# One kernel, four edits: GpSimd splits q and k, projections in one half turn, one dilation operation less, later transposes

## The chip, the cores and the metric

The kernel runs on one core of a Trainium2 chip. The time is the device time of one launch in microseconds (us); the median of several runs counts, and one further execution was recorded by the hardware profiler. The engines are named PE (matmul), PEld (its weight load), DVE (vector engine), ACT (scalar engine), POOL (GpSimd) and SP (which issues most DMAs). Each works through its own list of instructions in order and waits where one of them is not ready.

## What is computed

16 graphs of 1024 nodes with 128 features and a weighted 1024x1024 adjacency. Layer 0 is attention with 8 heads of 16, masked and weighted by the adjacency; layer 1 first thins the adjacency row by row ("dilation") and then runs three SAGE layers on it.

```python
# layer 0
h = relu(layernorm(x))
q, k, v = heads(h @ Wq.T + bq), heads(h @ Wk.T + bk), heads(h @ Wv.T + bv)
scores = where(adj == 0, -inf, q @ k.T / sqrt(16))
attn = softmax(scores) * adj
x = x + ((attn / (attn.sum(-1) + 1e-8)) @ v) @ Wo.T + bo
# layer 1, per graph, rows n in order
row = carry[n];  num = row.sum()
sf = (num + 1) // 2 if num > 10 else 1
rm = row & (cumsum(row) % sf == 0) & (num > 1)      # rows of nodes whose mask is set
carry[n] = row & ~rm;  carry[:, n] &= ~rm
# then, three times
agg = (adj_d @ h) / max(adj_d.sum(-1), 1)
o = agg @ Wr + h @ Wx + b;  h = batchnorm(relu(o / norm(o)))
x = x + concat(h1, h2, h3) @ Wl + bl
```

## The kernel before

**Two parts of one program.** `first_part` builds attention (a generator, `attention`) and dilation (a generator, `dilation`) and runs them interleaved in `beside_attention`; the SAGE layers follow in the loop over `L`, `b`, `c` below line 1275. PE, ACT and DVE execute in the order in which the Python code issues (a manual schedule), so where a line is called decides where it stands on its engine. Work for POOL and SP is issued in the same pass.

**A turn of attention** is (b, c, m): graph b, half c of the 512 query columns, block m of 128 key rows; 16 turns per graph, 256 in all. Each turn has two half turns g = 0 and 1, here called even and odd, four heads each. A half turn does, in this order:

1. `scores` (L596, L603): a mask product and the q-k products into two tiles of two banks, tag "sc". Float32 accuracy comes from q split in a rounded half `high` and a rest `low` (stacked in `qs`), and k in `ks` with alternate groups of 16 rows holding one or the other half.
2. even: `turn_over` (L547), the transposes of the adjacency block two turns ahead, into the one bank of tag "m".
3. `values` (L529, L534) for the half turn before, which needs its `w`.
4. the two exponentials `e` (L645) on ACT, one per score tile.
5. the two products `w = e * aT` (L650) on DVE.
6. even: the copy of the transposed block to `aT` (L550), which frees "m", and the mask `nomask` (L554).

**Steps beside it.** The next graph is prepared by generators kept in the list `beside`; each `yield` says where its next piece may go, and `go_on_with(kind)` at fixed places of a half turn lets the first generator that stands at that kind go on. `prepare(b)` does the layer norm, `turned` (transposes of h), and the projections: `key(c)`, `query(c)`, `value(c)`. `both_groups` (L349) makes a projection of two groups of heads, each with a matmul (L353) into tag "m" and a split:

```python
yield "end"                     # in prepare, ahead of key(0), query(0), key(1), query(1)
...
ps = where.tile([P, 512], F32, ...)        # both_groups, twice
nc.tensor.matmul(ps, wts[f"{name}{g}"], hT[:, c * HN : (c + 1) * HN], ...)
yield ("early", "evict")[g]
halves(c, g, ps)
if g == 0: yield "behind"
```

A step at "end" goes on at the close of an even half turn; "early" comes in the odd half turn ahead of `values`, "behind" after `values`, "evict" after the `w` products. For graph 0 the first two projections are made before the turns begin, with two banks. `query_halves` (L337, L338) and `key_halves` (L344, L345) read the projection out of PSUM twice: ACT writes the rounded half (for k it scales by `low_rows`, which is 1 for the rows of one kind and 0 for the others), DVE forms the rest from PSUM and that half.

**Dilation** works through 8 blocks of 128 rows, all graphs at once. At the end of a block, per graph: a running sum over pairs (`pair_sums`, L949, DVE); two ACT operations (L965) that turn it into distances from a threshold, one for even and one for odd places, written interleaved; a compare-and-maximum (L972) and a product with the row itself (L975), DVE; a maximum with earlier removals (L977); transposes (L956) and their copy (L958). The thresholds are small columns in `th` (L900 to L914).

**POOL** has the power of the layer norm (L302), the memset of `go_on` (L795), a small copy (L452), and the DMAs of the first rows (L504) and of the SAGE part.

**SAGE**: for each (L, b, c), `nodes` makes 64 sums in four pieces "sums", and the half before it (`before`) goes on between them with "scaled", "norm", "result", "transposed" (four transposes, L1225, and their copy, L1229). `turn_later` (L1344) decides whether "transposed" stands after the second or after the third piece. `judge` tests, once, that a sample is rounded alike by two engines.

Of the kernel before, what the change touches and what calls it, by code (L numbers as in the profile page):

```python
# [10 lines left out]
F32 = mybir.dt.float32  # L11
BF = mybir.dt.bfloat16
# [23 lines left out]
def swept(ctx: ExitStack, tc: tile.TileContext, t: dict, out: bass.AP, flag: bass.AP):  # L36
# [131 lines left out]
    def first_part(p1):  # L168
# [40 lines left out]
        wts |= {name: two_w[:, i, :] for i, name in enumerate(("q0", "q1", "k0", "k1"))}  # L209
        bqk = one.tile([P, 4, 2], F32, name="bqk")  # L210
        for i, name in enumerate(("L0_gnn_bq", "L0_gnn_bk")):
# [18 lines left out]
        def turn_weights():  # L230
            wps = ps_d.tile([P, 4, D], F32, name="wps", tag="d")
            for i in range(4):
                nc.tensor.transpose(wps[:, i, :], raw[:, i, :], ident)
            bps = ps_o.tile([P, HN], F32, name="bps", tag="acc0")
            for g in range(2):
                nc.tensor.matmul(
                    bps[:, 2 * g : 2 * g + 2], twice_ident[:, g, :], bqk[:, 0, :], start=True, stop=True
                )
            yield
            twofold(two_w[:, 2:4, :], wps[:, 3, :])  # L240
            twofold(two_w[:, 0:2, :], wps[:, 2, :])
            nc.vector.tensor_copy(one_w, wps[:, 0:2, :])
            nc.vector.tensor_copy(bqk[:, 1:3, :].rearrange("p g t -> p (g t)"), bps[:, 0:4])
            nc.vector.tensor_scalar(bqk[:, 3, :], bqk[:, 1:3, 1], low_rows, None, ALU.mult)
            yield
# [24 lines left out]
        free += 2 * (HN // 2 + 1)  # L270
        cx_home = both[:, free : free + HN]
        twice_ident = shared.tile([P, 2, P], F32, name="twice_ident", tag="s", bufs=2)
        twofold(twice_ident, ident)
# [38 lines left out]
        def prepare(b):  # L312
# [18 lines left out]

            def query_halves(c, g, ps):
                if g == 0:
                    qs.append(pool.tile([P, 2, 2, HN], F32R, name=f"q_{b}_{c}", tag="qM"))
                high, low = (qs[c][:, g, i, :] for i in range(2))
                bias = bqk[:, 1 + g, 0:1]
                nc.scalar.activation(high, ps, AF.Identity, bias=bias)  # L337
                nc.vector.scalar_tensor_tensor(low, ps, bias, high.bitcast(F32), ALU.add, ALU.subtract)  # L338

            def key_halves(c, g, ps):  # L340
                if g == 0:
                    ks.append(pool.tile([P, 2, HN], F32R, name=f"k_{b}_{c}", tag="kA", bufs=3))
                half = ks[c][:, g, :]
                nc.scalar.activation(half, ps, AF.Identity, bias=bqk[:, 3, g : g + 1], scale=low_rows)  # L344
                nc.vector.scalar_tensor_tensor(  # L345
                    half, ps, bqk[:, 1 + g, 1:2], half.bitcast(F32), ALU.add, ALU.subtract
                )

            def both_groups(name, halves, c, banks):  # L349
                for g in range(2):  # L350
                    where, tag = banks[g % len(banks)]
                    ps = where.tile([P, 512], F32, name=f"p{name}_{b}_{c}_{g}", tag=tag)
                    nc.tensor.matmul(  # L353
                        ps, wts[f"{name}{g}"], hT[:, c * HN : (c + 1) * HN], start=True, stop=True
                    )
                    yield ("early", "evict")[g]
                    halves(c, g, ps)
                    if g == 0:
                        yield "behind"
# [23 lines left out]
            if b == 0:  # L383
# [20 lines left out]
                yield from turned(1)  # L404
                yield "end"
                yield from key(1)
                yield True
                yield from value(1)
            else:
                yield from layer_norm_relu(h, xt, f"a{b}")  # L410
                for c in range(2):
                    yield True
                    yield from turned(c)
                yield "end"
# [4 lines left out]
                yield "end"  # L419
# [4 lines left out]
                yield "end"  # L424
                yield from key(1)
            yield "half 0"
            yield "end"
            yield from query(1)
# [93 lines left out]
        def attention():  # L522
# [87 lines left out]
            for i, (b, c, m) in enumerate(turns):  # L610
# [12 lines left out]
                for g in range(2):  # L623
                    scs = scores(i, g)
                    go_on_with(f"half {c}")
                    if g == 0:
                        go_on_with("first")
                        turning = turn_over(i + 2)
                        next(turning, None)
                    else:  # L630
                        twice_over = go_on_with("early")
                        if not twice_over:
                            go_on_with(True)
                    if late:
                        values(*late)
                        if g == 1 and twice_over:
                            go_on_with("behind")
                    elif g == 0:
                        go_on_with(True)
                    if (i, g) == (2, 0):  # L640
                        node_masks()
                    es, ws = [], []
                    for q in range(2):
                        e = pool.tile([P, 2, HN], F32, name=f"e_{b}_{c}_{m}_{g}_{q}", tag="e", bufs=4)
                        nc.scalar.activation(e, scs[q], AF.Exp, scale=1.0 / math.sqrt(HD))  # L645
                        es.append(e)
                    go_on_with("evict by VectorE")
                    for q in range(2):
# [11 lines left out]
                    go_on_with(False)  # L660
                    if g == 0 and next((kind for _, kind in beside if kind in (True, "end")), None) == "end":
                        go_on_with("end")
                    if i + g + 1 < len(turns):
# [8 lines left out]

        upto = one.tile([P, P], BF, name="upto")
        make_upper_triangular(nc, upto, 1.0, diag=True)
# [25 lines left out]
        def dilation():  # L700
# [84 lines left out]
            for k in range(NB):  # L785
# [29 lines left out]
                valid = shared.tile([P, B, P], BF, name=f"valid_{k}", tag="mr", bufs=4)  # L815
                cs = small.tile([P, 6, B], F32, name=f"cs_{k}", tag="cs", bufs=2)
                total, most, half, onw, last1, prev = (cs[:, i, :] for i in range(6))
# [81 lines left out]

                th = small.tile([P, 5, B], F32, name=f"th_{k}", tag="th", bufs=2)  # L900
                num, at_odd, off, allof, at_even = (th[:, i, :] for i in range(5))
                high = v[:, 3, :]
# [3 lines left out]
                nc.vector.tensor_scalar(high, num, 10.5, None, ALU.is_gt)  # L906
                nc.vector.scalar_tensor_tensor(allof, num, 1.5, high, ALU.is_gt, ALU.subtract)

                nc.vector.tensor_scalar(num, num, 0.5, 0.25, ALU.mult, ALU.add)
                nc.vector.tensor_scalar(num, num, MAGIC, MAGIC, ALU.add, ALU.subtract)  # L910
                nc.vector.tensor_scalar(at_odd, num, -3.0, None, ALU.mult)
                nc.vector.tensor_scalar(at_even, num, -3.0, 2.0, ALU.mult, ALU.add)
                nc.vector.scalar_tensor_tensor(off, num, 1.0, high, ALU.add, ALU.mult)
                nc.vector.tensor_scalar(off, off, -1.0, None, ALU.add)  # L914
                yield 2.0, 1
# [29 lines left out]
                for i in range(B + 2):  # L945
# [15 lines left out]
                    if b < B:  # L961
                        pairs[b] = shared.tile([P, 2, N], BF, name=f"pair_{k}_{b}", tag="mr", bufs=4)
                        wrs[b] = pairs[b][:, 0, :].bitcast(F16)
                        for t, at in enumerate((at_even, at_odd)):
                            nc.scalar.activation(  # L965
                                wrs[b][:, t::2], pair_sums[b % 2][:, t : t + HN], AF.Abs,
                                bias=at[:, b : b + 1], scale=2.0,
                            )
                    b = i - 1
                    if 0 <= b < B:  # L970
                        er = ers[b] = pairs.pop(b)[:, 1, :]
                        nc.vector.tensor_scalar(  # L972
                            er, wrs.pop(b), off[:, b : b + 1], allof[:, b : b + 1], ALU.is_equal, ALU.max
                        )
# [53 lines left out]
        def judge(sample):  # L1028
# [239 lines left out]
    with tc.manual_schedule(  # L1268
# [6 lines left out]
        for L in range(3):  # L1275
# [10 lines left out]
            for b in range(B):  # L1286
# [4 lines left out]
                for c in range(2):  # L1291
# [742 lines left out]
```

## Time and profile before

| | |
|---|---|
| median of 3 runs | 3463.39 us (3460.59 to 3468.24) |
| the profiled execution | 3457.88 us, of which the span of its instructions 3456.0 us |
| busy: PE, DVE, ACT, POOL | 3245.2, 3052.3, 2357.7, 165.0 us |
| granted TensorE clock | 0.991 |
| L650, product `w`, DVE | 1024 times, 1219 ns |
| L645, exponential `e`, ACT | 1024 times, 1022 ns |
| L353, projections, PE | 128 for k, 128 for q; 668 and 651 ns |
| L302, power, POOL | 33 times, shortest for 8 elements 1.64 us |

Busy times are sums over one engine; two engines can be busy at once. A row of the profile names the line, the engine, the operation and the tile that it writes and reads, with the shape. Matmul durations overlap, so that their mean is longer than the distance between two. A wait is an engine's idle time ahead of an instruction, put down to what came last; only a wait on the engine that is behind costs time.

### The profile page before, as it was taken

Reading aid. Unit: us, or ns where it says so; the run is one execution under the profiler, and the core shown is the slowest. Engines: PE = TensorE matmul, PEld = TensorE weight load, DVE = VectorE, ACT = ScalarE, POOL = GpSimd, SP = SyncE. Lnnn points to the kernel's source line nnn. Section 1 sums busy time; section 2 is a strip of 40 time slices with the busy share of each in tenths; the row PEclk is TensorE's granted clock in tenths of the full one; section 3 lists DMA queues with packets and bytes.
Section 4 is the critical chain, followed back from the end, with each engine's and each line's share of the span. In section 5 each row is a group of like instructions: output and inputs, shape, how many; then the busy total and the mean of one; then the engine's idle time right before and its main releaser. Section 6 shows DMA issues by size and latency. Waiting matters only on the chain. (4 is left out here: it accounts for less than half of the span.)

```text
span 3456.0 us, 86700 instructions
## 1 busy us (share of the span) xinstructions
PE 3245.2 (94%) x34987; PEld 1905.7 (55%) x34987; DVE 3052.3 (88%) x5410; ACT 2357.7 (68%) x3942; POOL 165.0 (5%) x253
## 2 busy tenths in 40 slices
PE   8998998999999899899999999999999899999997
PEld 3433333333343333333334334336999899999997
DVE  8888988988898898998999999997888799988887
ACT  7699789779879978977986996895323343432334
POOL 2000000000000000000000000001000000000000
PEclk9999999999999999999999999999999999999999
DMA  7356447537645735754773684577999799989997
GB/s 237 108 170 184 138 130 211 149 121 211 186 132 177 232 121 156 231 168 138 223 218 112 204 256 128 152 220 265 342 336 334 278 352 351 349 327 349 351 352 237
DMA packets 650124, 772.30 MB, mean 223 GB/s; under 512 B 173264, under 2 KB 569168, under 8 KB 637424
## 3 DMA queue, kind: packets, MB, share of 16 engines
q1 hardware_dynamic: 632672, 708.58, 63.1%
q0 software_dynamic: 15456, 57.30, 4.9%
q8 instruction: 276, 4.52, 0.6%
q14 instruction: 136, 1.11, 0.1%
q10 hardware_dynamic: 1584, 0.79, 0.1%
HBM read 508.50 MB, written 157.29 MB: 193 GB/s over the span
## 5 line engine op out<-in xcount | busy, mean ns | idle before, releaser
L650 DVE TENSOR_TENSOR w<-e,aT 128x1024 f32<-128x1024 f32 x1024 | 1205.9, 1219 | 135.3 <-ACT e L645 134.1
L645 ACT ACTIVATE e<-sc 128x1024 f32<-128x1024 f32 x1024 | 991.2, 1022 | 230.1 <-PE sc L603 229.6
L1188 PE MATMUL pg<-y,aT 128*128 128x128 f32 (+1 forms) x6144 | 730.5, 275 | 0.0
L1188 PEld LDWEIGHTS pg<-y,aT 128*128 128x128 f32 x6144 | 708.7, 192 | 0.0
L529 PE MATMUL acc<-w,both 128*32 128x512 f32 x4096 | 619.6, 610 | 4.5 <-DVE w L650 2.4
L534 PE MATMUL acc<-e,eps 128*32 128x512 f32 x4096 | 598.3, 594 | 0.0
L147 DVE SCALAR_TENSOR_TENSOR aT<-mr,aT 128x1024 f32<-128x1024 bf16 x384 | 458.8, 1217 | 0.0
L603 PE MATMUL sc<-q,k 32*128 32x512 f32 x4096 | 379.8, 445 | 0.0
L596 PE MATMUL sc<-nomask,never 32*32 32x512 bf16 x8192 | 272.8, 386 | 53.7 <-ACT e L645 46.8
L534 PEld LDWEIGHTS acc<-e,eps 128*32 128x32 f32 x4096 | 155.4, 111 | 299.5 <-issue 289.7
L596 PEld LDWEIGHTS <-never 32*32 32x32 bf16 x8192 | 86.8, 88 | 395.7 <-issue 376.8
L1211 ACT ACTIVATE sq<-o 128x512 f32<-128x512 f32 x96 | 60.6, 631 | 356.9 <-DVE o L1206 356.9
L1229 ACT COPY hT<-pt 128x512 f32<-128x512 f32 x96 | 56.3, 586 | 266.4 <-PE pt L1225 257.9
L603 PEld LDWEIGHTS sc<-q,k 32*128 32x128 f32 x4096 | 155.7, 183 | 117.1 <-issue 116.9
L547 PE MATMUL pa<-ident,a 128*128 128x128 f32 x1024 | 168.3, 287 | 46.6 <-DVE k L345 20.4
L965 ACT ACTIVATE pair<-both,th 128x512 f16<-128x512 f16 x256 | 204.8, 876 | 2.4 <-DVE both L949 2.3
L529 PEld LDWEIGHTS acc<-w,both 128*32 128x32 f32 x4096 | 97.3, 108 | 155.4 <-DVE w L650 77.3
L547 PEld LDWEIGHTS pa<-ident,a 128*128 128x128 f32 x1024 | 107.6, 141 | 135.2 <-issue 56.3
L554 ACT ACTIVATE nomask<-aT 128x512 bf16<-128x512 f32 x256 | 161.5, 631 | 8.1
L1206 DVE SCALAR_TENSOR_TENSOR o<-pg,rdeg,mine 128x128 f32<-128x128 f32 x384 | 108.1, 344 | 56.2 <-PE pg L1188 53.0
L949 DVE TENSOR_TENSOR_SCAN both<-rk 128x513 f16<-128x513 bf16 x128 | 155.9, 1218 | 0.0
L550 ACT COPY aT<-pa 128x512 f32<-128x512 f32 x256 | 152.5, 596 | 4.9 <-PE pa L547 4.5
(240 smaller groups left out, 4056.5 us busy)
## 6 DMA issues: line engine op xcount, KB each, us to landing
aT<-aT_d SPq DMA_DIRECT2D x94, 2048.0 KB, 9.7
mr<-mr_d SPq DMA_DIRECT2D x188, 512.0 KB, 6.0
aT_d<-aT SPq DMA_DIRECT2D x256, 256.0 KB, 3.8
a<-in_adj SPq DMA_DIRECT2D x253, 256.0 KB, 3.3
ad<-in_adj SPq DMA_DIRECT2D x112, 512.0 KB, 4.4
nomask<-nomask SPq DMA_DIRECT2D x512, 96.0 KB, 2.5
nomask<-nomask SPq DMA_DIRECT2D x512, 64.0 KB, 2.7
nomask<-nomask SPq DMA_DIRECT2D x512, 32.0 KB, 2.6
```

What stands on the lines that cost most here:

```text
L147: nc.vector.scalar_tensor_tensor(part, mrs[h][:, j : j + 2, :].rearrange("p j n -> p (j n)"), 0.0, part, ALU.is_equal, ALU.mult)
L529: nc.tensor.matmul(acc[g][32 * j : 32 * j + 32, :], v1[:, m, (2 * j + g) * HW : (2 * j + g) * HW + 32], ws[j // 2][:, j % 2, :], start=(m ...
L534: nc.tensor.matmul(acc[g][32 * j : 32 * j + 32, :], eps8, es[j // 2][:, j % 2, :], start=False, stop=(m == NB - 1),)
L547: nc.tensor.transpose(pa[:, k * P : (k + 1) * P], a[:, k, :], ident)
L554: nc.scalar.activation(nomask[:, 0, :], aT[:, 0, :], AF.Relu, bias=1.0, scale=-1e38, accum_out=zeros[:, i : i + 1])
L596: nc.tensor.matmul(scs[j // 2][to : to + 32, j % 2, :], never[rows, rows], nomask[rows, j, :], start=True, stop=False, tile_position=(32 * ...
L603: nc.tensor.matmul(scs[j // 2][:, j % 2, :], ks[m // HB][rows, g, mm], qs[c][rows, g, half, :], start=False, stop=(half == 1), tile_positi ...
L645: nc.scalar.activation(e, scs[q], AF.Exp, scale=1.0 / math.sqrt(HD))
L650: nc.vector.tensor_tensor(w, es[q], aT.to_broadcast([P, 2, HN]), ALU.mult)
L949: nc.vector.tensor_tensor_scan(pair_sums[b % 2], row[:, 0::2], row[:, 1::2], 0.0, ALU.add, ALU.add)
L965: nc.scalar.activation(wrs[b][:, t::2], pair_sums[b % 2][:, t : t + HN], AF.Abs, bias=at[:, b : b + 1], scale=2.0,)
L1188: nc.tensor.matmul(pg[:, i // 2, at : at + width], aT[:, j, i * P : (i + 1) * P], y[:, j, :width], start=(j == 0), stop=(j == NB - 1),)
```

## The change

- **Projections.** ACT makes one plain copy with bias, `whole` (one buffer), of each projection; the two halves are then made from it by the engine given to `halves`: POOL where "m" is the only bank, DVE for the first two projections of graph 0. For q these are a copy to the rounded type and a subtraction, for k a product with `low_rows` and a subtraction. The fourth column of `bqk` goes.
- **Placing.** The kind "end" goes; a projection begins like other steps in the odd half turn, after `scores`. "early" now stands behind the first of the two exponentials, in every half turn; `values` and "behind" follow the second. Both groups of a projection fall into one half turn.
- **Dilation.** ACT writes the even and the odd distances as two contiguous halves, with a per-row factor `twos` in place of 2.0; the thresholds are built from `twos` such that a row removed as a whole needs no maximum; compare and product with the row are one `scalar_tensor_tensor` that reads and writes every second element. `cs` and `th` have one buffer instead of two.
- **SAGE.** `turn_later` holds in layer 0 for both halves.
- `upto` lies in spare room of the tile `both`, and the sample in `judge` is rounded by POOL instead of ACT.

```diff
-            def query_halves(c, g, ps):
+            def whole(name, g, ps, bias):
+                x = small.tile([P, HN], F32, name=f"whole_{name}_{b}_{g}", tag="whole", bufs=1)
+                nc.scalar.activation(x, ps, AF.Identity, bias=bias)
+                return x
+
+            def query_halves(c, g, ps, engine):
...
-                bias = bqk[:, 1 + g, 0:1]
-                nc.scalar.activation(high, ps, AF.Identity, bias=bias)
-                nc.vector.scalar_tensor_tensor(low, ps, bias, high.bitcast(F32), ALU.add, ALU.subtract)
-
-            def key_halves(c, g, ps):
+                x = whole(f"q{c}", g, ps, bqk[:, 1 + g, 0:1])
+                engine.tensor_copy(high, x)
+                engine.tensor_tensor(low, x, high.bitcast(F32), ALU.subtract)
+
+            def key_halves(c, g, ps, engine):
...
-                nc.scalar.activation(half, ps, AF.Identity, bias=bqk[:, 3, g : g + 1], scale=low_rows)
-                nc.vector.scalar_tensor_tensor(
-                    half, ps, bqk[:, 1 + g, 1:2], half.bitcast(F32), ALU.add, ALU.subtract
-                )
+                x = whole(f"k{c}", g, ps, bqk[:, 1 + g, 1:2])
+                engine.tensor_scalar(half, x, low_rows, None, ALU.mult)
+                engine.tensor_tensor(half, x, half.bitcast(F32), ALU.subtract)
...
-                    halves(c, g, ps)
+                    halves(c, g, ps, nc.gpsimd if len(banks) == 1 else nc.vector)
...
-                yield "end"
+                yield True
                 yield from key(1)
...
                     else:
-                        twice_over = go_on_with("early")
-                        if not twice_over:
-                            go_on_with(True)
-                    if late:
-                        values(*late)
-                        if g == 1 and twice_over:
-                            go_on_with("behind")
-                    elif g == 0:
                         go_on_with(True)
-                    if (i, g) == (2, 0):
-                        node_masks()
                     es, ws = [], []
                     for q in range(2):
                         e = pool.tile([P, 2, HN], F32, name=f"e_{b}_{c}_{m}_{g}_{q}", tag="e", bufs=4)
                         nc.scalar.activation(e, scs[q], AF.Exp, scale=1.0 / math.sqrt(HD))
                         es.append(e)
+                        if q == 0:
+                            go_on_with("early")
+                    if late:
+                        values(*late)
+                        go_on_with("behind")
+                    elif g == 0:
+                        go_on_with(True)
+                    if (i, g) == (2, 0):
+                        node_masks()
...
-                    if g == 0 and next((kind for _, kind in beside if kind in (True, "end")), None) == "end":
-                        go_on_with("end")
...
-                cs = small.tile([P, 6, B], F32, name=f"cs_{k}", tag="cs", bufs=2)
+                cs = small.tile([P, 6, B], F32, name=f"cs_{k}", tag="cs", bufs=1)
...
-                nc.vector.scalar_tensor_tensor(allof, num, 1.5, high, ALU.is_gt, ALU.subtract)
+                nc.vector.scalar_tensor_tensor(twos, num, 1.5, high, ALU.is_gt, ALU.subtract)
+                nc.vector.tensor_scalar(twos, twos, -2.0, 2.0, ALU.mult, ALU.add)
...
-                nc.vector.tensor_scalar(at_odd, num, -3.0, None, ALU.mult)
-                nc.vector.tensor_scalar(at_even, num, -3.0, 2.0, ALU.mult, ALU.add)
+                nc.vector.scalar_tensor_tensor(at_odd, num, -1.5, twos, ALU.mult, ALU.mult)
+                nc.vector.tensor_tensor(at_even, at_odd, twos, ALU.add)
                 nc.vector.scalar_tensor_tensor(off, num, 1.0, high, ALU.add, ALU.mult)
-                nc.vector.tensor_scalar(off, off, -1.0, None, ALU.add)
+                nc.vector.scalar_tensor_tensor(off, twos, -0.5, off, ALU.mult, ALU.add)
...
-                                wrs[b][:, t::2], pair_sums[b % 2][:, t : t + HN], AF.Abs,
-                                bias=at[:, b : b + 1], scale=2.0,
+                                wrs[b][:, t * HN : (t + 1) * HN], pair_sums[b % 2][:, t : t + HN], AF.Abs,
+                                bias=at[:, b : b + 1], scale=twos[:, b : b + 1],
...
-                        nc.vector.tensor_scalar(
-                            er, wrs.pop(b), off[:, b : b + 1], allof[:, b : b + 1], ALU.is_equal, ALU.max
+                        nc.vector.scalar_tensor_tensor(
+                            er.rearrange("p (i t) -> p t i", t=2), wrs.pop(b).rearrange("p (t i) -> p t i", t=2),
+                            off[:, b : b + 1], rk(b, 2, N + 2).rearrange("p (i t) -> p t i", t=2),
+                            ALU.is_equal, ALU.mult,
                         )
-                        nc.vector.tensor_tensor(er, er, rk(b, 2, N + 2), ALU.mult)
...
-            nc.scalar.copy(rounded[:, 0], sample)
+            nc.gpsimd.tensor_copy(rounded[:, 0], sample)
...
-                    turn_later = before and c == 0 and b > 0
+                    turn_later = before and (c == 0 or L == 0)
```

More of the change, by code (lines that the diff above doesn't have):

```diff
@@ L209, in first_part @@
         wts |= {name: two_w[:, i, :] for i, name in enumerate(("q0", "q1", "k0", "k1"))}
-        bqk = one.tile([P, 4, 2], F32, name="bqk")
+        bqk = one.tile([P, 3, 2], F32, name="bqk")
         for i, name in enumerate(("L0_gnn_bq", "L0_gnn_bk")):
@@ L243, in turn_weights @@
             nc.vector.tensor_copy(bqk[:, 1:3, :].rearrange("p g t -> p (g t)"), bps[:, 0:4])
-            nc.vector.tensor_scalar(bqk[:, 3, :], bqk[:, 1:3, 1], low_rows, None, ALU.mult)
             yield
@@ L271, in first_part @@
         cx_home = both[:, free : free + HN]
+        upto_home = both[:, free + HN : free + HN + P // 2].bitcast(BF)
         twice_ident = shared.tile([P, 2, P], F32, name="twice_ident", tag="s", bufs=2)
@@ L413, in prepare @@
                     yield from turned(c)
-                yield "end"
+                yield True
                 yield from key(0)
@@ L418, in prepare @@
                 yield "half 1"
-                yield "end"
+                yield True
                 yield from query(0)
@@ L423, in prepare @@
                 yield from value(1)
-                yield "end"
+                yield True
                 yield from key(1)
             yield "half 0"
-            yield "end"
+            yield True
             yield from query(1)
@@ L670, in attention @@
             ready["last"] = conclude(*done)
-        upto = one.tile([P, P], BF, name="upto")
+        upto = upto_home
         make_upper_triangular(nc, upto, 1.0, diag=True)
@@ L896, in dilation @@
                             nc.tensor.matmul(g, final[:, b, :], vb[:, 1, b, 0:1], start=False, stop=True)
-                th = small.tile([P, 5, B], F32, name=f"th_{k}", tag="th", bufs=2)
-                num, at_odd, off, allof, at_even = (th[:, i, :] for i in range(5))
+                th = small.tile([P, 5, B], F32, name=f"th_{k}", tag="th", bufs=1)
+                num, at_odd, off, twos, at_even = (th[:, i, :] for i in range(5))
                 high = v[:, 3, :]
```

## The prediction

> **What bounds the kernel now.** First the busy times by stage, with the stretch borders read from the timeline: up to 2385 us attention and dilation run interleaved, after that the three SAGE layers.
>
> ```profile
> 20.00:2385.00 2365.00, 2200.00 (x25948) 877.79 (x25947) 2134.93 (x3520) 1979.18 (x3151) 108.71 (x142) 0.99 0.58 175
> 2385.00:3456.00 1071.00, 1033.65 (x9015) 1022.20 (x9014) 906.27 (x1839) 370.77 (x777) 46.25 (x85) 0.98 0.92 331
> ```
>
> Columns: stretch, length, then busy us of PE, PEld, DVE, ACT, POOL, clock, DMA share, GB/s. In the second stage PE is busy 97% and nothing of it is touched but one transpose position. In the first PE (93%) and DVE (90%) both carry it, ACT has 84%, and POOL is empty (5%). [...]I take DVE as the first bound and ask where DVE and PE still wait. The waits of that stage answer:
>
> ```profile
> DVE w L650 <- ACT e L645: 134.1, 188, 2.8
> PEld pk L353 <- ACT aT L550: 60.5, 31, 3.6
> PEld pq L353 <- ACT aT L550: 45.4, 31, 2.6
> DVE k L345 <- ACT k L344: 34.8, 34, 3.3
> PEld pa L547 <- DVE k L345: 33.6, 31, 1.2
> PEld pa L547 <- DVE q L338: 33.1, 31, 1.2
> DVE q L338 <- ACT q L337: 18.4, 25, 2.3
> ```
>
> (total us, times, longest.) Nearly all but the first line belong to the q and k projections: the first of two matmuls waits at the end of an even half turn for ACT to empty the one "m" bank, and the next turn's transposes (`pa`) wait for DVE to empty it again. What that costs shows in the period between the `w` pairs (L650 starts in the timeline, means over batches 1 to 15, by the m of the turn, period / DVE busy, us):
>
> ```
> m      even half    odd half     carries
> 0      6.25/4.68    5.67/5.17    key(1), and the copies of acc
> 1      5.05/4.68    5.60/5.41    query(1)
> 12     4.86/3.81    5.08/4.46    key(0)
> 14     5.04/3.93    5.06/4.46    query(0)
> 2,3,5  4.27/4.16    4.60/4.35    no projection
> 8      4.64/4.11    4.53/4.17    the copies of acc
> ```
>
> Elsewhere DVE is 97% busy in even half turns; in those with a projection it idles 0.4 to 1.6 us.
>
> **Projections: removed.** The rows that are replaced (line, operation, count, busy us, mean ns):
>
> ```profile
> L344 ACT ACTIVATE k<-pk,bqk,low_rows 128x512 fp32r<-128x512 f32 x64 | 50.0, 781 | 39.1 <-PE pk L353 39.1
> L345 DVE SCALAR_TENSOR_TENSOR k<-pk,bqk,k 128x512 fp32r<-128x512 f32 x64 | 47.8, 747 | 37.1 <-ACT k L344 37.0
> L338 DVE SCALAR_TENSOR_TENSOR q<-pq,bqk,q 128x512 fp32r<-128x512 f32 x64 | 47.7, 745 | 18.4 <-ACT q L337 18.4
> L337 ACT ACTIVATE q<-pq,bqk 128x512 fp32r<-128x512 f32 x64 | 44.1, 690 | 40.7 <-PE pq L353 40.7
> ```
>
> Of 128 groups the first four (batch 0) go to DVE with two instructions each; 124 leave it. The next DVE start follows such an operation by 0.66 us, so DVE loses 124 x 0.67 = 83 us, 1.34 per pair of groups, 62 pairs. ACT keeps one evict per group at the 690 of L337 and saves 64 x 0.09 = 6.
>
> **Projections: moved.** Both groups now run in one odd half turn: first matmul behind the scores, its evict between the two exponentials, second matmul behind the values, its evict last. "m" was emptied half a turn before, so both kinds of bank wait go. Even half turns should fall to their neighbours: 6.25 to 4.64, and 5.05, 4.86, 5.04 to about 4.2, which is 1.6+0.9+0.7+0.8 = 4.0 us per batch. Projection steps issue no DMA.
>
> **Projections: added on POOL.** Two instructions per group, 248 in all. No POOL row of this size exists. The memsets of L795 (128x2048, 1805 ns) and L796 (128x16, 197 ns) give 0.17 us + 0.8 ns per element: 0.58 us for the one-input step. For two inputs I count the element cost twice, 0.99; the Trainium skill (GPSIMD Engine Reference, Performance versus the Vector engine) measures 4497 ns at 2048 elements, by its 2.6 cycles an estimated 1.17. I take 1.0. Then what they do to DVE. The trace has one reading POOL instruction beside a busy DVE:
>
> ```profile
> 1272.91 1.22 DVE L885 TENSOR_TENSOR hit<-w,at 128x2048 bf16<-128x2048 f16 x1
> 1273.14 2.48 POOL L302 TENSOR_TENSOR rs_b<-rs_b,minus_half 128x8 f32<-128x8 f32 x1 [31.10 <-DVE rs_b L301]
> 1274.04 2.36 DVE L650 TENSOR_TENSOR w<-e,aT 128x1024 f32<-128x1024 f32 x2
> ```
>
> L302 takes 1.64 at its shortest. Here it took 0.84 more, just what L885 had left; then the `w` pair ran at its usual length beside it. So POOL waits for a DVE operation with two SBUF inputs, and DVE was not held. The rule speaks against this change: the Trainium skill (SBUF — State Buffer, Who interferes with whom) has a DVE instruction with two SBUF inputs and a GpSimd instruction that reads SBUF exclude each other, the loser blocked for the whole instruction. The row contradicts "whole instruction", but its 8 elements are read at once; 512 are read throughout. By the row the hold H of a pair (four POOL instructions) is 0; by the rule 2 x (0.58+1.17) = 3.5 us, more than the 1.34 saved. I take 2.0: the two subtractions hold DVE fully, the two one-input steps fall where DVE waits anyway, because the evict between the exponentials makes the second one 0.69 us later.
>
> Pair time after = DVE busy before - 1.34 + H + 0.3 of waits that stay, but never under what is left without any hold: the even half turn of the neighbours plus an odd one of 5.0 (before 5.06 to 5.67; 0.6 us of matmul more, 1.34 of DVE less), 9.6 at m=0 and 9.2 else:
>
> ```
> m     before  DVE busy  H=0   H=2.0  H=3.5
> 0     11.92   9.85      9.6   10.8   12.3
> 1     10.65   10.09     9.2   11.05  12.55
> 12    9.94    8.27      9.2   9.25   10.75
> 14    10.10   8.39      9.2   9.35   10.85
> sum   42.61             37.2  40.45  46.45
> ```
>
> Times 15.5 batches: -84, **-33** and +60 us.
>
> **The new buffer.** `whole` has one buffer, so the second evict waits on ACT until POOL has read the first copy twice: 0.58 + 1.0 + a mean POOL wait of 0.4 before each (L302's excess over 1.64) = 2.4 us after the first evict; the second matmul is ready 1.5 after it. ACT stands 0.9 us, and the next exponential is queued behind. In a pair with H=2.0 DVE is behind by more than that, so I count nothing; without that cover it costs 0.4 to 0.9 per pair (25 to 55 us). Also behind POOL's new work: the power L302, which stands between the last copy and the last subtraction of query(1) (DVE's L304 waits for it one half turn later), the memset of go_on, and in batch 0 six first-row loads; +2 us in all.
>
> **Dilation.** L972 (536 ns) and L975 (693) become one operation; start of the first to start of the follower is 1.30 us. L765 with two bf16 inputs takes 1083 at 896 elements, so 1.22 at 1024, 1.26 with the same dependence: 128 x 0.04 = -5. Bounds: 1.14 as between independent operations (-20), and +20 if reading every second element cost DVE what it seems to cost ACT. ACT's L965 (876 ns) writes halves contiguously but takes a second pointer; L1152, that form, takes 805: 256 x 0.07 = 18 us of ACT, worth nothing, since DVE never idled for L965. One more tiny operation per block: 8 x 0.17 = +1. Single buffers for `cs`, `th`: their readers are done a block earlier, nothing.
>
> **Later turn.** In layer 0 the transposes of odd halves move behind one more set of sums. `PEld pt L1225 <- DVE o L1221: 4.6, 15` in that layer goes: -4; nothing is due soon behind it. The copy that goes to POOL in the final test runs once: 0 to 3.
>
> **Sum.** -33 + 2 - 5 + 1 - 4 = -39 on the profiled 3457.88 (span 3456.0): 3419. The median of the runs shown is 5.5 higher; I put the time at **3420**.
>
> **Rivals.**
> - **No hold** (H=0), chance 0.2: -84, +25 for the stand on ACT that no DVE backlog covers, -6 for the rest: about 3393. For it: the undelayed `w` beside L302. Against: that reads 8 elements.
> - **Full hold, slower**, 0.25: each POOL instruction shuts DVE out for its length, H=3.5: +60-6, about 3512. The pairs break even near H=2.5, so it decides from 0.64 us of hold per POOL instruction. For it: POOL demonstrably waits for DVE, and at m=0 and 1 DVE has little idle time to give.
> - **The `whole` wait replaces the bank wait**, 0.15: POOL, waiting for DVE twice, needs 4 us, ACT stands 2.5 us, and the even half turn's gain goes back: about 3455.
> - The forecast, 0.4: 3395 to 3445.
>
> **Numbers.** The range 3375 to 3500 holds the forecast, the no-hold and the buffer case; the full hold spreads over 3470 to 3530, and a bit over half of it is left out. Faster: all of no hold, 0.37 of the forecast's 0.4, half of the buffer case: 0.64. Within 0.2% (7 us, about what can be told from no change) 0.08; slower 0.28.
>
> **What would show it.** POOL rows of 0.6 and 1.0 us plus waiting; even half turns at m=1, 12, 14 near 4.2; no wait of `pk`, `pq` for `aT`; `w` rows longer than 1219 ns, or idle DVE put down to POOL, if it is held; `whole` waiting for POOL on ACT. POOL rows over 1.5 us with odd half turns over 6 would make it wrong.

## The result, and the profile after

The changed kernel takes **3510.82 us** (median of 4 runs, 3508.95 to 3518.39), the kernel before on the same chip 3464.73 (4 runs): a ratio of 1.0138, 95% interval 1.0119 to 1.0157. It is slower by some 46 us. The forecast of 3420 is missed by 91 us, and the range of 3375 to 3500 too. The profiled execution of the changed kernel took 3518.39 us with a span of 3516.5 at a granted clock of 0.984.

The stages first, by the view that the prediction began with. The border now lies at 2443 us, because the last product `w` ends at 2439.2 instead of 2378.4. Columns: stretch, length, busy us of PE, PEld, DVE, ACT, POOL, clock, DMA share, GB/s.

```profile
20.00:2443.00 2423.00, 2247.25 (x25921) 884.89 (x25921) 2178.06 (x3275) 1964.42 (x3151) 486.08 (x389) 0.98 0.57 170
2443.00:3516.00 1073.00, 1034.22 (x9041) 1025.88 (x9039) 909.79 (x1842) 371.16 (x777) 47.62 (x87) 0.98 0.91 331
```

All the loss is in the first stage, 58 us longer; the SAGE stage is as long as it was. POOL has gone from 109 to 486 us there. DVE, which was to be relieved, is busy 43 us more.

Where that comes from stands in the groups of operations on POOL and DVE (busy us, mean ns of one, idle time before it):

```profile
L350 POOL TENSOR_SCALAR k<-whole_k,low_rows 128x512 fp32r<-128x512 f32 x62 | 121.9, 1966 | 562.6 <-ACT whole_k L334 562.6
L343 POOL TENSOR_TENSOR q<-whole_q,q 128x512 fp32r<-128x512 f32 x62 | 115.1, 1857 | 3.8
L351 POOL TENSOR_TENSOR k<-whole_k,k 128x512 fp32r<-128x512 f32 x62 | 83.7, 1350 | 4.9
L342 POOL CAST q<-whole_q 128x512 fp32r<-128x512 f32 x62 | 55.8, 901 | 237.3 <-ACT whole_q L334 237.3
```

```profile
L653 DVE TENSOR_TENSOR w<-e,aT 128x1024 f32<-128x1024 f32 x1024 | 1261.4, 1269 | 199.8 <-ACT e L639 198.3
...
L974 DVE SCALAR_TENSOR_TENSOR pair<-pair,th,rk 128x1024 bf16<-128x1024 f16 x128 | 200.4, 1566 | 0.0
```

The POOL steps take 0.9 to 2.0 us where 0.58 and 1.0 were counted. The products `w` have grown from 1219 to 1269 ns in the mean; of the 1024 none took over 1.3 us before, and now 84 do, 27 of them about 2.3. All 84 run beside one of the POOL steps: DVE is held inside its instruction. And DVE waits 198.3 us for exponentials, before 134.1.

Why the exponentials come late is in the waits (us in total, times, longest; the last line is that of the attention stage alone):

```profile
DVE w L653 <- ACT e L639: 198.3, 219, 4.2
...
ACT whole_k L334 <- POOL k L351: 82.8, 31, 4.3
ACT whole_q L334 <- POOL q L343: 72.4, 29, 3.8
PEld pa L551 <- ACT whole_k L334: 57.1, 31, 3.5
PEld pa L551 <- ACT whole_q L334: 47.1, 30, 2.3
...
PEld pk L357 <- ACT aT L554: 9.1, 15, 0.8
```

The bank waits of `pk` and `pq` for `aT` are nearly gone, but in nearly every pair ACT now stands 2.6 us in front of the second evict until POOL has read the first copy twice. Behind that evict stand the next exponentials on ACT and the next turn's transposes (`pa`), which need the bank: they wait 104 us, where before they waited 67 for DVE to empty it. One pair in the timeline (start, duration, engine, line; idle time and its cause in brackets):

```profile
1046.60 0.69 ACT L334 ACTIVATE whole_k<-pk,bqk 128x512 f32<-128x512 f32 x1
...
1047.39 1.87 POOL L350 TENSOR_SCALAR k<-whole_k,low_rows 128x512 fp32r<-128x512 f32 x1 [24.64 <-ACT whole_k L334]
...
1049.35 1.28 POOL L351 TENSOR_TENSOR k<-whole_k,k 128x512 fp32r<-128x512 f32 x1
...
1050.66 0.69 ACT L334 ACTIVATE whole_k<-pk,bqk 128x512 f32<-128x512 f32 x1 [2.46 <-POOL k L351]
1051.24 1.93 ACT L639 ACTIVATE e<-sc 128x1024 f32<-128x1024 f32 x2
...
1051.44 1.56 POOL L350 TENSOR_SCALAR k<-whole_k,low_rows 128x512 fp32r<-128x512 f32 x1 [0.82 <-ACT whole_k L334]
...
1052.30 3.44 DVE L653 TENSOR_TENSOR w<-e,aT 128x1024 f32<-128x1024 f32 x2 [2.24 <-ACT e L639]
...
1053.09 1.56 POOL L351 TENSOR_TENSOR k<-whole_k,k 128x512 fp32r<-128x512 f32 x1
```

Read downwards it is one chain: first evict, two POOL steps, second evict after 2.46 us of standing, exponentials, and DVE, idle for 2.24 us, begins its `w` pair; that pair then takes 3.44 us in place of 2.35, while the second group's POOL steps run beside it (1051.44 to 1054.65).

The periods between `w` pairs, read as in the prediction (period / DVE busy, us, means over batches 1 to 15):

```
        before                     after
m       even half   odd half       even half   odd half
0       6.25/4.68   5.67/5.17      4.56/3.96   7.16/5.44
1       5.05/4.68   5.60/5.41      4.74/4.64   6.77/5.88
12      4.86/3.81   5.08/4.46      3.53/3.14   6.94/5.03
14      5.04/3.93   5.06/4.46      3.73/3.29   7.15/5.46
```

The even half turns fell as forecast. The odd ones took it back: a pair takes 1.94 us more than DVE's busy time (44.58 less 36.84 over four pairs, divided by four), where 0.3 was counted. The even half turns just behind a pair, at m=2 and m=13, rose too, from 4.17 and 3.79 to 5.06 and 4.15: POOL is still at work on the pair there and holds `w`.

### The profile page after: what moved, and what is told of

The parts are those of the page before. It is cut to its first block, busy times and chain, and to the rows that moved or that the text cites. A ratio compares the mean times of both kernels' runs of the same rounds, so it can differ in the third digit from the quotient of the medians.

```text
span 3516.5 us, 86951 instructions
## 1 busy us (share of the span) xinstructions
PE 3292.3 (94%) x34987; PEld 1916.4 (54%) x34987; DVE 3099.3 (88%) x5169; ACT 2343.1 (67%) x3941; POOL 543.8 (15%) x502
## 5 line engine op out<-in xcount | busy, mean ns | idle before, releaser
L653 DVE TENSOR_TENSOR w<-e,aT 128x1024 f32<-128x1024 f32 x1024 | 1261.4, 1269 | 199.8 <-ACT e L639 198.3
L533 PE MATMUL acc<-w,both 128*32 128x512 f32 x4096 | 647.0, 620 | 12.9 <-DVE w L653 10.0
L538 PE MATMUL acc<-e,eps 128*32 128x512 f32 x4096 | 624.0, 605 | 0.0
L147 DVE SCALAR_TENSOR_TENSOR aT<-mr,aT 128x1024 f32<-128x1024 bf16 x384 | 458.9, 1217 | 0.0
L600 PE MATMUL sc<-nomask,never 32*32 32x512 bf16 x8192 | 280.7, 386 | 67.4 <-ACT e L639 61.8
L350 POOL TENSOR_SCALAR k<-whole_k,low_rows 128x512 fp32r<-128x512 f32 x62 | 121.9, 1966 | 562.6 <-ACT whole_k L334 562.6
L974 DVE SCALAR_TENSOR_TENSOR pair<-pair,th,rk 128x1024 bf16<-128x1024 f16 x128 | 200.4, 1566 | 0.0
L967 ACT ACTIVATE pair<-both,th 128x512 f16<-128x512 f16 x256 | 195.0, 818 | 4.1 <-DVE both L951 4.1
```

The lines of the kernel that those rows point to most:

```text
L147: nc.vector.scalar_tensor_tensor(part, mrs[h][:, j : j + 2, :].rearrange("p j n -> p (j n)"), 0.0, part, ALU.is_equal, ALU.mult)
L533: nc.tensor.matmul(acc[g][32 * j : 32 * j + 32, :], v1[:, m, (2 * j + g) * HW : (2 * j + g) * HW + 32], ws[j // 2][:, j % 2, :], start=(m ...
L538: nc.tensor.matmul(acc[g][32 * j : 32 * j + 32, :], eps8, es[j // 2][:, j % 2, :], start=False, stop=(m == NB - 1),)
L600: nc.tensor.matmul(scs[j // 2][to : to + 32, j % 2, :], never[rows, rows], nomask[rows, j, :], start=True, stop=False, tile_position=(32 * ...
L653: nc.vector.tensor_tensor(w, es[q], aT.to_broadcast([P, 2, HN]), ALU.mult)
L967: nc.scalar.activation(wrs[b][:, t * HN : (t + 1) * HN], pair_sums[b % 2][:, t : t + HN], AF.Abs, bias=at[:, b : b + 1], scale=twos[:, b : ...
```

## The experiments

Two theories stood against each other. **W**: the wait of the second evict for the one `whole` buffer makes the kernel slow. **H**: POOL's reading holds DVE, buffer or not. A third, **D**, put it on the dilation. The kernel before ran beside each group, at 3460.3 to 3461.0 us, so times of different groups can be set side by side to about a microsecond; beside the changed kernel itself it stood at 3464.7, and a few us of each difference to 3510.82 are uncertain. For the space of the second buffer or a spare tile, e1, e6, e9, e10, e11 and e14 leave out the record of the denominators and its test (L452 before, 13 us on POOL, which has room); what that alone is worth was not measured.

**A second `whole` buffer (e1).**

```diff
-  x = small.tile([P, HN], F32, name=..., tag="whole", bufs=1)
+  x = small.tile([P, HN], F32, name=..., tag="whole", bufs=2)
```

> The changed kernel (3511 us) with two buffers for whole; room comes from leaving out the record rden of the denominators and its test. Theory W (ACT stands in the odd half turn until POOL has read the single copy, 155 us of waits in the trace of the changed kernel): those waits go, odd half turns with a projection fall from 7.0 to about 5.5, time about 3420 to 3440. Theory H (POOL's reading holds DVE, so DVE sets the pair): DVE is as busy as before, time 3485 to 3510. Theory D (the joined dilation operation, 1566 instead of 536+693 ns): no change, 3505 to 3515.

Measured 3458.73 us (20 runs; ratio to before 0.9989, 0.9982 to 0.9995), so the one buffer costs **52 us**. (e3 below, which keeps the one buffer and ran beside e1, stands 53 us over it.) Its waits:

```profile
DVE w L651 <- ACT e L637: 128.2, 162, 3.4
...
ACT whole_q L333 <- PE pq L356: 54.4, 35, 6.3
ACT whole_k L333 <- PE pk L356: 33.7, 35, 2.1
```

No `whole` waits for POOL, and DVE's wait for exponentials has fallen from 198.3 to 128.2, by 70 us, while DVE is held more than in the changed kernel (busy 3119.3 against 3099.3). W names the largest part, but its 3420 to 3440 was not reached: something else costs 20 to 40 us more.

**The halves by ACT and DVE again, all else changed (e2).**

```diff
-  x = whole(f"q{c}", g, ps, bqk[:, 1 + g, 0:1])
-  engine.tensor_copy(high, x)
-  engine.tensor_tensor(low, x, high.bitcast(F32), ALU.subtract)
+  nc.scalar.activation(high, ps, AF.Identity, bias=bias)
+  nc.vector.scalar_tensor_tensor(low, ps, bias, high.bitcast(F32), ALU.add, ALU.subtract)
   (k likewise)
```

> The changed kernel with the halves made by ACT and DVE out of PSUM as before; placing, dilation and later turn as changed. W and H both say that all of the loss goes: both name POOL. Even half turns stay near 4.0 as in the changed kernel, odd ones return to 5.1 to 5.6: about 3400 to 3430, below the kernel before. D says that the loss stays: about 3500.

Measured **3434.59 us**, ratio 0.9927 (0.991 to 0.9944): faster than the kernel before, and the fastest of all that ran, if 5 us above the range expected: its even half turns with a projection take 4.7 to 5.7 us, not 4.0. Making the halves on POOL costs 76 us against that, 52 by the one buffer and 24 even with two.

**The dilation alone, both ways (e3, e4).** e3 is the changed kernel with the dilation operations of before, e4 the kernel before with those of the change.

> The changed kernel with the dilation operations as before (compare with maximum, then product; interleaved writing by ACT). D: DVE has 43 us less in that operation and 16 less in its followers, about 3455. W and H: these sit in half turns without a projection, where DVE has little slack but the periods hardly moved: 3495 to 3510.

> The kernel before with only the dilation operations of the change. D: +45 to +60 us, about 3515. W and H: +0 to +15 us, 3464 to 3480. The joined operation takes 1566 ns here too if its stride and not POOL makes it long; 1217 ns if POOL did.

Measured 3511.69 (ratio 1.0141) and 3461.38 (0.9997, 0.9988 to 1.0006). D falls. The joined operation in e4, where no projection work of POOL lies beside it:

```profile
L973 DVE SCALAR_TENSOR_TENSOR pair<-pair,th,rk 128x1024 bf16<-128x1024 f16 x128 | 179.7, 1404 | 0.0
```

That is 0.19 us over the 1217 expected. Reading and writing every second element is the likely reason; no run tests it apart. DVE is busy 22 us more in e4, at no cost in time.

**The placing alone (e5), the later turn alone (e8).** e5 is e2 with the dilation and the turn of before.

```diff
(e8)
-  turn_later = before and c == 0 and b > 0
+  turn_later = before and (c == 0 or L == 0)
```

> Only the placing of the projections is changed: both groups in one odd half turn, halves by ScalarE and VectorE as before, the dilation and the turn of before. Theory W (the placing gains, the wait for the one whole buffer took it back): the gain of e2_no_pool is that of the placing, so 3425 to 3445, even half turns with a projection near 4.6, no bank wait of a projection. Theory P (the gain of e2_no_pool came from the later turn or the dilation, the placing is worth nothing): 3455 to 3465.

> The kernel before with the changed turn_later alone. My step of -4 us: 3455 to 3460. Nothing: 3459 to 3463. If the later turn were a large part of what e2_no_pool gains (Theory P): 3440 to 3450.

Measured 3442.02 (0.9944, 0.9928 to 0.9961) and 3456.47 (0.9985, 0.9973 to 0.9997), against 3461.0 before: the placing gains 19 us, the later turn 4.5. Theory P falls. e5's even half turns with a projection came to 4.8 to 5.8, not to 4.6. The waits on the bank that stay there:

```profile
PEld pk L354 <- DVE k L346: 41.3, 31, 2.4
PEld pq L354 <- DVE q L339: 35.2, 31, 2.4
PEld pa L548 <- DVE k L346: 34.6, 31, 1.2
PEld pa L548 <- DVE q L339: 33.2, 31, 1.2
```

As long as DVE empties the bank, placing both groups in one half turn lets the second matmul wait for the first group's split, instead of for `aT`.

**POOL work that nobody waits for (e6, e10, e11).** On e5, behind each group, a copy and a subtraction (e6), the copy alone (e10) or a subtraction alone (e11), into a spare tile:

```diff
   halves(c, g, ps)
+  nc.gpsimd.tensor_copy(spare, made.bitcast(F32))
+  nc.gpsimd.tensor_tensor(spare, made.bitcast(F32), spare.bitcast(F32), ALU.subtract)
```

Here `made` is the finished half; in e11 the second operand is `hT`.

> e5_placing_alone with two more GpSimd instructions behind each group of the projections (a copy and a subtraction of 128x512 from the finished half into a spare tile that nobody reads; so nobody waits for GpSimd). It prices the hold alone. Hold real at the 0.27 us per GpSimd instruction that the lengthened VectorE rows of the changed kernel show: 248 x 0.27 = 67 us more VectorE time, 40 to 67 us over e5_placing_alone. No hold that counts (only the buffer wait cost anything): 0 to 10 us over it. Full hold (2.0 to 3.5 us per pair): 120 to 220 over it.

> e6_spare_pool without its spare subtractions: 124 GpSimd copies of 128x512 that nobody reads, on e5_placing_alone. e6 lost 78.6 us over e5. Theory S (the hold comes from the subtractions with two inputs, a copy reads through and holds nobody, as my forecast had it): 0 to 8 us over e5 (3442 to 3450). Theory E (each reading GpSimd instruction holds VectorE by its own length): in the ratio of their durations, 1037 to 1798 ns, 29 us over e5 (3465 to 3475).

> e6_spare_pool without its spare copies: 124 GpSimd subtractions of 128x512 from two tiles, on e5_placing_alone. Theory S: 65 to 79 us over e5 (3507 to 3521). Theory E: about 50 over e5 (3487 to 3497). If the cost lies in the pair coming back to back and not in either: both single kinds together well under 79.

Measured 3520.57, 3450.80 and 3500.52: 78.6, 8.8 and 58.5 us over e5. e6 lies between the ranges given for the priced hold and for the full one. The groups of e11, two on POOL and the product `w`:

```profile
L361 POOL TENSOR_TENSOR spare_k<-k,hT 128x512 fp32r<-128x512 f32 x62 | 110.0, 1774 | 869.4 <-DVE k L345 848.4 <-DMA nomask<-nomask 16.9 <-DVE pair L984 1.9
L361 POOL TENSOR_TENSOR spare_q<-q,hT 128x512 fp32r<-128x512 f32 x62 | 94.4, 1523 | 316.8 <-ACT q L337 301.8 <-DMA a<-in_adj 13.6 <-DMA aT_d<-aT 1.4
```

```profile
L652 DVE TENSOR_TENSOR w<-e,aT 128x1024 f32<-128x1024 f32 x1024 | 1257.9, 1269 | 103.2 <-ACT e L638 101.6
```

The same of e10, the copies of k and `w`:

```profile
L361 POOL CAST spare_k<-k 128x512 fp32r<-128x512 f32 x62 | 68.9, 1111 | 879.5 <-DVE k L345 875.6 <-DVE pair L984 1.9 <-DVE v L868 1.9
...
L652 DVE TENSOR_TENSOR w<-e,aT 128x1024 f32<-128x1024 f32 x1024 | 1218.5, 1231 | 114.8 <-ACT e L638 113.7
```

The mean of `w` is 1269 beside subtractions, 1231 beside copies. DVE is busy 74 us more with 124 subtractions, 0.60 each, and 14 us more with 124 copies, 0.11 each. The hold is real, most of it comes from the subtractions with two inputs, and 11 us of e6 belong to the two together. Neither theory is met in full: e10 lies 0.8 us above S's range and 20 under the 29 of E; e11, 58.5, lies between S's 65 and E's 50. And a copy does hold DVE: in e10 35 of the 1024 `w` take over 1.3 us, each begun while a copy ran, up to 1.63. So a copy holds too, but for less (0.4 us where a subtraction cost a `w` up to 1.1) and less often. POOL pays as well: its subtraction takes 1649 ns in the mean here, 1261 at its shortest in the changed kernel, and half of the k copies take about 1.47 where the shortest takes 0.61.

**The POOL halves alone (e9).** The kernel before with `whole` (one buffer) and the POOL steps, the groups still half a turn apart.

> The kernel before with the halves made by GpSimd from whole (one buffer) and nothing else: the two groups stay half a turn apart, as before. The record of the denominators and its test are left out for the space. Theory W: with 4 us between the two evicts, whole is free at the second and ScalarE doesn't stand; VectorE loses 83 us and gets about 65 back as hold, the m bank is free one VectorE operation earlier: 3430 to 3455. Theory H (the hold, not the buffer, makes the change slow): 3480 to 3510.

Measured 3514.86 us, ratio 1.0152 (1.0135 to 1.0169): as slow as the whole change. That is against W, and 5 us above the range of H. ACT's waits:

```profile
ACT whole_k L333 <- POOL k L350: 22.1, 14, 2.3
...
ACT whole_q L333 <- POOL q L342: 5.0, 2, 3.5
ACT whole_q L333 <- POOL k L350: 2.1, 2, 1.2
```

Only 18 stands with 29 us in sum are left, but DVE is busy 43 us more than before (3095.6 against 3052.3) though it lost 124 instructions, and `PEld pk` still waits 59.5 us for `aT`. The first evict still comes at the close of an even half turn. So the buffer is not all: with the hold (79 us in e6, where nobody waits for POOL) and no gain from the placing, the kernel is as slow with little standing. The periods say where: at m=12 and 14 DVE has 0.6 us less to do in the even half turns, yet these still take 4.85 and 4.91 us (4.86 and 5.04 before), while the held odd ones rise from 5.08 and 5.06 to 5.99 and 5.81.

**A shorter POOL chain (e12).**

```diff
-  engine.tensor_scalar(half, x, low_rows, None, ALU.mult)
+  engine.tensor_copy(half, x)
```

> The changed kernel with the first GpSimd step of the keys a plain copy instead of the product with low_rows (the keys' upper rows then hold the residual too, so the scores are others). The copy takes 0.6 us at its shortest where the product takes 1.56, so the second evict of a key pair should wait 0.9 us less. Theory W (the time lies in ScalarE's stand for whole): the wait of whole_k for GpSimd falls from 83 to about 55 us and the time by 10 to 25, to 3485 to 3500. Theory H (hold): 31 pairs x 2 x 0.9 us less of reading, at the 0.4 us that VectorE grew per GpSimd us, 10 to 25 us less too, but with w rows nearer to 1219. Neither (the product costs no more than a copy once it is waiting for VectorE): 3506 to 3512.

Measured 3505.78, 5 us under the changed kernel (ratio 1.0124, 1.0106 to 1.0142, against 1.0138, so hardly clear of noise): a miss for W and H, just at "neither". POOL's groups show why:

```profile
L351 POOL TENSOR_TENSOR k<-whole_k,k 128x512 fp32r<-128x512 f32 x62 | 112.2, 1809 | 4.7
...
L350 POOL CAST k<-whole_k 128x512 fp32r<-128x512 f32 x62 | 55.6, 897 | 561.8 <-ACT whole_k L334 561.8
```

The first step fell from 1966 to 897 ns, the subtraction behind it rose from 1350 to 1809: presumably it now meets the `w` that the longer product had let pass, which no run tests. The wait of `whole_k` for POOL fell by 10 us only.

**The first evict behind both exponentials (e13 on e2, e14 on e1).**

```diff
-  if q == 0:
+  if q == 1:
       go_on_with("early")
```

> e2_no_pool (no GpSimd halves) with the first evict of a pair behind both exponentials instead of between them. In e2_no_pool VectorE still waits 104 us for exponentials and 51 for the evicts. Theory B (the evict between the exponentials makes the second one, and with it w, 0.7 us later, which my sum held for free): 62 pairs x 0.3 to 0.6 us less, 3400 to 3420. Theory M (the second matmul of the pair and the next turn's transposes need the bank early, so a later evict is paid there): 3440 to 3460.

> e1_two_buffers (GpSimd halves, two whole buffers) with the first evict behind both exponentials. Theory B: as before this run, 3425 to 3445 against its 3458.7. Theory M: 3460 to 3480, for here too the bank comes free later.

Measured 3478.69 and 3465.66, 44 and 7 us slower than e2 and e1. Theory B falls; M is right in direction, and in e13 19 us short. In e13 the second matmul waits for the bank:

```profile
PEld pk L354 <- DVE k L346: 63.4, 31, 2.9
...
PEld pq L354 <- DVE q L339: 52.9, 31, 2.5
```

That is 116 us where e2, with the early evict, has 75 (40.0 and 35.4) in the same two rows. The evict is better placed between the exponentials than behind them.

The parts, set together:

| step | from | us |
|---|---|---|
| placing | e5 less before | -19 |
| later turn | e8 less before | -4.5 |
| dilation | e4 less before | +0.5 |
| the three together | e2 less before | -26 |
| halves by POOL, two buffers | e1 less e2 | +24 |
| one buffer for `whole` | after less e1 | +52 |
| sum of the last three | | +50 |

The last three add up to the whole change by construction, as each run is subtracted once: +50 against the 3461 of the experiments, +46 against the 3464.7 that ran beside the changed kernel. The first three are independent of their joint run: -23 against -26.

## Why the prediction was wrong

**"The new buffer ... I count nothing" failed.** It put ACT's stand, counted from the end of the second matmul, at 0.9 us per pair and covered it with DVE's backlog. Both halves are wrong. From the end of the first evict to the end of the second POOL step the trace has 3.4 us in the mean where 2.4 were taken, because the steps counted as 0.58 and 1.0 take 901+1857 ns for q and 1966+1350 for k. The second matmul ends 1.9 us after that evict (1.5 taken), so the buffer holds ACT 1.6 us beyond it. (The 155.2 us over 60 times, 2.6 us each, count from ACT's instruction before; with two buffers 88.1 us remain, for the matmul itself.) And there is no cover: the exponentials queued behind the stand feed DVE, which then waits (70 us more than with two buffers). Price: 52 us, at the upper end of the 25 to 55 named for the case without cover. The rival "the `whole` wait replaces the bank wait" had the mechanism and the 2.5 us of standing; it added 36 us for it, too little, to a base that was itself 39 us too fast.

**The pair sum failed too: "0.3 of waits that stay", and all of the hold inside the pair.** Even with the wait for the buffer gone, e1 stands at 3458.7, 39 us above the forecast. Us per batch, period / DVE busy, both half turns together:

```
turns               before         forecast (H=2.0)   e1
m=0, 1, 12, 14      42.6 / 36.6    40.45 / 39.2       41.4 / 37.6
m=2                 8.5 / 8.2      as before          9.4 / 9.3
m=13                8.5 / 7.1      as before          8.8 / 8.1
the other ten       88.2           as before          88.0
```

First, the pairs idle 0.97 us each, not 0.3. The 0.3 was read at m=2, 3 and 5, and "elsewhere DVE is 97% busy" holds there but not everywhere: before, the even half turns at m=8, 10, 13 and 15 are at 84 to 89%, and the whole turns at m=8, 13 and 15, which have no projection, idle 0.9, 1.4 and 1.2 us. The pairs of e1 idle about as much as such neighbours: 1.0 at m=0, 0.1 at m=1, 1.4 and 1.3 at m=12 and 14. Second, DVE is less busy inside the pairs than forecast, since about a quarter of the hold falls behind them: at m=2 and 13 it is busy 1.0 us more, and at m=2 it had no idle time to give (e2, without POOL, keeps 4.16 and 3.77 us in these even half turns, e1 has 5.17 and 4.29). Over 15.5 batches the pairs lie 15 us above the forecast, m=2 and 13 19 us above before; the remaining 5 us were not traced. Why the late turns idle at all was not looked into. The even half turns did reach their neighbours (4.56, 4.74, 3.53, 3.73 against 4.64 and 4.2), but in part as a shift within the pair. e13 and e14 show that a later first evict does not win this back. The sum also gives 3424 on the median of 3463.4, not the 3420 that was written.

**The hold was right in size, less so in place.** DVE is busy 47.0 us more than before. It lost 95.5 us (L338 and L345, before), less 5 for batch 0, and the strided dilation adds 22 (e4), so the hold is 47 + 90.5 - 22 = 115 us, 1.86 per pair against the 2.0 taken, between the ends 0 and 3.5. That the subtractions hold far more than the copies is what e10 and e11 show; that part of it falls behind the pair is shown above. The weighing of row and rule behind it was wrong in one point: from the power L302, with 8 elements, I read that DVE isn't held at all, but with 512 elements 33 of e11's 1024 `w` took about 2.3 us, 1.1 more than the usual 1.22 and so nearly a whole subtraction, as the Trainium skill has it (SBUF — State Buffer, Who interferes with whom). It is the mean, 0.60 per subtraction, that is smaller, since in other cases POOL is the one that waits, or the two don't meet. That the time came out at the "full hold" rival's 3512 is luck: its 3.5 us of hold per pair is not what was measured.

**POOL durations.** The copy was right (0.61 at its shortest against 0.58). The subtraction takes 1.26 where I took 1.0, and the 1.17 estimated from the Trainium skill (GPSIMD Engine Reference, Performance versus the Vector engine) was nearer. The product with `low_rows` was counted as a one-input step like the copy and takes 1.56 at its shortest. In e12, which has a copy there, the time is 5 us lower, so this last error matters little.

**Right:** the waits of `pk`, `pq` for `aT` (60.5 us for `pk` before, 9.1 after in the attention stage), though not the other bank wait, that of the transposes, which grew from 67 to 104 us behind the standing evict (21 with two buffers); the later turn, -4 expected and -4.5 measured; the dilation's ACT row (818 ns, 805 expected) and its lack of effect. The dilation operation was missed, 1404 ns (1566 with POOL beside it) for 1217, but at no cost in time. The sign that would make the forecast wrong, POOL rows over 1.5 us with odd half turns over 6, came about.

## What to carry to other kernels

A new single buffer between two engines is a wait of the producer on the slowest reader; price it with what stands behind the producer in its queue, and don't take a backlog elsewhere as its cover when that queue feeds the backlog. Read the idle time that stays from the turns which resemble the changed ones, not from the busiest. Moving two-input work from VectorE to GpSimd saved 90 us of VectorE instructions here and gave 115 us back as held ones, so here such a move would have needed either copies alone (0.11 us of hold each) or a place where VectorE idles. Price the parts of a change one by one: the placing and the later turn were worth 26 us (e2, 3434.6 us), and the part meant to relieve VectorE cost 76.

## What the runs showed of the hardware

- On GpSimd a product with a per-row scalar takes 1.56 us at its shortest for 128x512 float32, a copy of the same size 0.61 and a subtraction of two tiles 1.26; VectorE took 0.49 for the same product and 0.69 for the same subtraction in batch 0.
- GpSimd and VectorE hold each other inside the instruction: beside subtractions `w` of 1.22 us takes up to 2.3, beside copies up to 1.63 (e10); the subtraction on GpSimd goes from 1.26 to as much as 3.1 (q in the changed kernel).
- A `scalar_tensor_tensor` on 1024 two-byte elements with every second element read and written takes 1404 ns.
